# A third level of Strassen for one of the seven small products of a half product, in groups 1 to 3

## The chip, the cores and the metric

The kernel runs on one core of one Trainium2 chip. The metric is the device time of one execution in microseconds. The kernel before was timed three times on the chip: 819.81, 819.81 and 819.62 us, median 819.81 us. A profile of one further execution gives the start and length of every instruction.

## The reference

The input `x` has 4 x 1024 rows of 1024 floats. The rows are normalised, and two things are made of them: a gated recurrence along the rows of a sequence (its gate is `sigmoid(xn @ gate_w.T + gate_b)`), and a network whose outputs are added, by their top-2 expert numbers 0 to 7, into eight rows only. As `silu(0)` is 0, all other rows of the result are `x`, and the recurrence is needed for the first sequence alone.

```python
xn = _layernorm(x, axis=-1)
# attention-like part
g   = sigmoid(einsum('btd,ed->bte', u, gate_w) + gate_b);  u_g = u * g
y   = c * s + d_eff * u_g                    # s: cumulative sum along the sequence; d_eff: needs the mean of u_g
# network part, on all 4096 rows of xn
gates = top-2 of softmax(xr @ wr.T), renormalised
h = silu(xr @ w1.T);  h = silu(h @ w3.T);  h = h @ w2.T
out = out.at[indices_k[:, k]].add(gates[:, k:k+1] * h)
# result
return x + y * silu(out)
```

Nearly all the arithmetic lies in three products with a 1024 x 1024 matrix: `w1` and `w3` for all 4096 rows, `gate_w` for the first 1024 rows. All of it is in float32.

## The kernel before

**Groups and half products.** The 4096 rows ("tokens") are worked in four groups of 1024, numbered `sb` = 0 to 3. Each group has a product with `w1` (kind `u`), then a product with `w3` (kind `m`); group 0 also has the one with `gate_w` (kind `g`). A 1024 x 1024 x 1024 product is made by one level of Strassen (the Winograd form) as seven products of 512 x 512 x 512; the source calls each a `Half` and names it by its number `i`. `u` takes them in the order 1, 2, 5, 6, 7, 4, 3 and `m` in the order 1, 5, 6, 2, 7, 4, 3.

**Seven steps of a half.** Each half is made by a second level of Strassen, so by seven products of 256 x 256 x 256. One such product is one step on TensorE: four matmuls with 128 x 128 weights and 256 moving columns (function `small`, line 869). In float32 the profile records each matmul as two weight loads and two matmul records, so a step is eight records. `Half.step(n)` (line 919) runs step n. Steps 0, 2, 4 and 6 add into one PSUM bank, X; steps 1 and 5 into another, Z; step 3 makes its product alone in the bank Y. X and Z have two buffers each, Y has one (lines 104 to 106), and with the others all eight PSUM banks are in use.

**Reading the banks out.** After most steps VectorE adds the bank, as far as it has been summed, to a 128 x 512 quarter of the output block in SBUF: `first` (line 904) for quarters 0, 3, 1 and 2 after steps 0, 1, 2 and 6, and `more` (line 913) for quarters 0, 3 and 1 after steps 3, 4 and 5. In halves 1 and 5 the reads of `first` are copies on ScalarE. Step 3 is `go(Y, A[:, 1], t[:, 2], True, True)` and then `self.more(0, Y)`. In halves 6 and 7 every finished quarter is followed by one more VectorE addition between output blocks (`whole`, line 1005), and a finished quarter of a final block goes through SiLU on ScalarE (`done`).

**Operands.** The sums that the second level needs are made by GpSimd on the token side (`left_sums`, 128 x 512 subtractions and additions); the weight sums were made in group 0, stored to DRAM, and are loaded again for groups 1 to 3 (`load_kept` 1 MB, `load_kept_sum` 256 KB each). The token sums of the first level (`s1` to `s4`) run on GpSimd for `u` in groups 1 to 3 and on VectorE for `m`. While the `m` product of group 1 or 2 runs, VectorE also normalises the tokens of the next group, in 16 operations of 128 x 1024 (`norm`, line 407). All 128 x 512 operands live in a ring of `NQ` = 18 tiles ("quarters"), taken from the front and given back at the end; 1 MB blocks live in a ring of 20.

**Order.** The order of work on every engine is written out by the program. Each half has a starting place S, seven places after the half before it; its step n runs at place S + 2n. So steps 4, 5 and 6 of the half before fall at S + 1, S + 3 and S + 5, between the steps 0 to 3 of this one, and each place holds one step. Other work is put on a list with `at(place, function)`; whatever is due at a place is issued before the step of that place (`run_todo`, lines 186 to 201, and the loop at line 1421). Each engine then keeps exactly that order, and waits when an operand or a buffer is not ready. The route of the next group's tokens (`route`, line 439: two transposes, VectorE maxima, a sigmoid on ScalarE, VectorE comparisons) is spread over such places during the first halves of `u`.

Of the kernel before, what the change touches and what calls it, by code (L numbers as in the profile page):

```python
# [10 lines left out]
F32 = mybir.dt.float32  # L11
# [3 lines left out]
ALU = mybir.AluOpType  # L15
AX = mybir.AxisListType
P = 128
Q = 256
# [4 lines left out]
def kernel(  # L23
# [55 lines left out]
    class Pinned:  # L79
# [15 lines left out]
    nc = tc.nc  # L95
    pe, dve, act, pool, sync = (
        Pinned(e) for e in (nc.tensor, nc.vector, nc.scalar, nc.gpsimd, nc.sync)
    )
# [7 lines left out]
    ps_y = ctx.enter_context(tc.tile_pool(name="ps_y", bufs=1, space=bass.MemoryType.PSUM))  # L106
# [15 lines left out]
            if self.uses == 0:  # L122
                self.home.append(self.tile)

    NB, NQ = 20, 18
    IDLE = 13
    blocks = deque(
        const.tile([P, 4, 2 * Q], F32, tag=f"b{i}", name=f"b{i}") for i in range(NB)
# [8 lines left out]
    def quarter(uses=1):  # L137
        return Held(quarters, uses)
# [47 lines left out]
    def at(place, f, *args):  # L186

        seq[0] += 1
        heapq.heappush(todo, (place, seq[0], f, args))
# [8 lines left out]
    def resume(p, g):  # L198
        step = next(g, None)
        if step is not None:  # L200
            at(p + step, resume, p + step, g)
# [14 lines left out]
    start = {}  # L216
# [301 lines left out]
    kept = {}  # L518
    op_t = {}
# [14 lines left out]
    def keep_quarter(name, i, j, o):  # L534
        d = dramp.tile([P, 2 * Q], F32, tag=f"{name}_{i}_{j}", name=f"{name}_{i}_{j}")
        sync.dma_start(d, o.tile)
        kept[name, i, j] = d
        o.drop()
# [177 lines left out]
    def first_w3():  # L716
# [48 lines left out]
    S_OF = {  # L765
        1: (0, 0),
        2: (0, 1),
        4: (1, 1),
        5: "s1",
        6: "s2",  # L770
        3: "s4",
        7: "s3",
    }
    left = {}
# [91 lines left out]
                yield 2 * (A_AT[j + 1] - A_AT[j])  # L866


    def small(ps, A, B, start, stop, rows_first):

        for mt in range(2):
            for kt in range(2):
                w, m = (A, B) if rows_first else (B, A)
                pe.matmul(
                    ps[:, mt * Q : (mt + 1) * Q],
                    w[:, kt * Q + mt * P : kt * Q + (mt + 1) * P],
                    m[:, kt * Q : (kt + 1) * Q],
                    start=(start and mt == 0 and kt == 0),
                    stop=(stop and mt == 1 and kt == 1),
                    skip_group_check=True,  # L880
                )
# [3 lines left out]
    class Half:  # L885
# [30 lines left out]
        def whole(self, q):  # L916
            whole(self.kind, self.sb, self.i, q)

        def step(self, n):
            if n == 0:  # L920
                self.begin()
            A, t = self.A, self.t
            ts = [op_ts.get((self.kind, self.sb, self.i, j)) for j in range(4)]
            s = [left_q.get((self.src, self.sb, self.i, j)) for j in range(4)]

            def go(ps, a, b, start, stop):
                small(ps, a, b, start, stop, self.rows_first)

            if self.plain:

                q = ((0, 1, 2, 3) if self.i == 1 else (0, 3, 1, 2))[n // 2]
                ps = self.X if n // 2 % 2 == 0 else self.Z
                go(ps, A[:, q // 2 * 2 + n % 2], t[:, n % 2 * 2 + q % 2], n % 2 == 0, n % 2 == 1)
                if n % 2:
                    self.first(q, ps)
            elif n == 0:
                go(self.X, A[:, 0], t[:, 0], True, False)
                self.first(0, self.X)
            elif n == 1:
                go(self.Z, s[0].tile, ts[0].tile, True, False)  # L940
                self.first(3, self.Z)
                s[0].drop()
                ts[0].drop()
            elif n == 2:
                go(self.X, s[1].tile, ts[1].tile, False, False)
                self.first(1, self.X)
                s[1].drop()
                ts[1].drop()
            elif n == 3:
                Y = ps_y.tile([P, 2 * Q], F32, tag="Y", name=f"Y_{self.tag}")  # L950
                go(Y, A[:, 1], t[:, 2], True, True)
                if (self.kind, self.i) == ("g", 1):
                    at(Y_AT, self.more, 0, Y)
                else:
                    self.more(0, Y)
            elif n == 4:
                go(self.X, s[2].tile, ts[2].tile, False, False)
                self.more(3, self.X)
                s[2].drop()
                ts[2].drop()  # L960
            elif n == 5:
                go(self.Z, s[3].tile, t[:, 3], False, True)
                self.more(1, self.Z)
                s[3].drop()
            elif n == 6:
                go(self.X, A[:, 3], ts[3].tile, False, True)
                self.first(2, self.X)
                self.whole(2)
                ts[3].drop()
            if n == (7 if self.plain else 6):  # L970
                self.A.drop()
                t.drop()
# [265 lines left out]
    for kind, sb, i, plain in line:  # L1238
        h = Half(kind, sb, i, plain)
        halves.append(h)  # L1240
        S = start[kind, sb, i]
        n = 2 if sb == 0 and kind == "u" and i not in PLAIN_G else 1
        if kind != "g" and not plain:
            at(S + 2 - 8, left_sums, kind, sb, i, n)
        if kind != "g" and sb > 0:
            at(S - 10, load_kept, kind, sb, i)
            for j in range(4):
                at(S + 2 * T_AT[j] - 9, load_kept_sum, kind, sb, i, j)

    for sb in range(NS):  # L1250
        n = 2 if sb == 0 else 1
# [252 lines left out]
```

## Time and profile before

| what | us |
|---|---|
| median of 3 runs (lowest, highest) | 819.81 (819.62, 819.81) |
| span of the profiled execution | 817.9 |
| what lies around the span, against the median | 1.9 |
| one step on TensorE, 8 records, distance to the next step | 1.73 |
| VectorE, PSUM bank Y + SBUF, 128 x 512, mean of one | 0.69 |
| VectorE, `whole` and first-level sums, 128 x 512, mean of one | 0.93 |
| VectorE, normalising, 128 x 1024, mean of one | 1.21 |
| GpSimd, 128 x 512 sum, mean of one | 1.31 to 1.36 |
| load of a 256 KB weight sum, issue to landing, median | 4.5 |

The profiled execution's own time is known by its span; the three timed runs lie 1.7 to 1.9 us above that. A page of the profile gives the busy time of each engine, the chain of work that ended last, and the costliest groups of instructions; the timeline lists instructions of one engine in order of time, as "start, length, engine, line, operation, output<-inputs, shape, how many in a row". Nearly all instructions are recorded by one helper (line 89), so they are told apart by their tiles: `b` is a 1 MB block, `q` a quarter, `X_u`, `Z_m`, `Y_m` and so on the PSUM banks of the halves, `bc` the normalisation's factors.

### The profile page before, as it was taken

Reading aid. Unit: us, or ns where it says so; the run is one execution under the profiler, and the core shown is the slowest. Engines: PE = TensorE matmul, PEld = TensorE weight load, DVE = VectorE, ACT = ScalarE, POOL = GpSimd, SP = SyncE. Lnnn points to the kernel's source line nnn. Section 1 sums busy time; section 2 is a strip of 40 time slices with the busy share of each in tenths; the row PEclk is TensorE's granted clock in tenths of the full one; section 3 lists DMA queues with packets and bytes.
Section 4 is the critical chain, followed back from the end, with each engine's and each line's share of the span. In section 5 each row is a group of like instructions: output and inputs, shape, how many; then the busy total and the mean of one; then the engine's idle time right before and its main releaser. Section 6 shows DMA issues by size and latency. Waiting matters only on the chain.

```text
span 817.9 us, 11299 instructions
## 1 busy us (share of the span) xinstructions
PE 810.6 (99%) x4085; PEld 696.5 (85%) x4085; DVE 509.7 (62%) x868; ACT 263.8 (32%) x458; POOL 496.1 (61%) x398
## 2 busy tenths in 40 slices
PE   8999999999999999999999999999999999999997
PEld 7888888888888878888888788888888788888885
DVE  6886598765588524764985235666983246667643
ACT  1245126877232237341022065421122021220111
POOL 2799896967999394744547453755448454465300
PEclk9999999999999999999999999999999999999999
DMA  9946619465978947629955875559666365555700
GB/s 338 421 175 232 230 47 357 171 246 160 411 267 309 345 174 293 241 103 385 376 179 210 332 279 190 187 206 426 242 244 257 104 219 203 196 180 195 283 14 2
DMA packets 55927, 192.88 MB, mean 236 GB/s; under 512 B 6480, under 2 KB 9792, under 8 KB 44224
## 3 DMA queue, kind: packets, MB, share of 16 engines
q1 hardware_dynamic: 55552, 191.61, 63.5%
q8 instruction: 33, 0.54, 0.3%
q10 hardware_dynamic: 320, 0.54, 0.2%
q14 instruction: 22, 0.18, 0.1%
HBM read 169.01 MB, written 39.87 MB: 255 GB/s over the span
## 4 chain that ended last, share of the span: by engine, by line
PE 98%; DMA 1%; DVE 0%; ACT 0%; issue 0%; SPq 0%
PE X_u L89 24%; PE X_m L89 24%; PE Z_u L89 12%; PE Z_m L89 12%; PE X_g L89 6%; PE Y_m L89 6%; PE Y_u L89 6%; PE Z_g L89 3%; PE acc L89 2%; PE plT L89 2%; PE Y_g L89 1%; DMA b<-in_x 1%; PE pp L89 0%; DVE bn L89 0%; PE accB L89 0%; PE ta L89 0%
## 5 line engine op out<-in xcount | busy, mean ns | idle before, releaser
L89 POOL TENSOR_TENSOR q<-b 128x512 f32<-128x512 f32 x154 | 203.0, 1331 | 193.7 <-PE X_m L89 48.0
L89 ACT ACTIVATE b<-b 128x512 f32<-128x512 f32 (+1 forms) x152 | 105.3, 696 | 298.1 <-DVE b L89 291.6
L89 POOL TENSOR_TENSOR q<-b,q 128x512 f32<-128x512 f32 x98 | 133.1, 1361 | 7.2 <-issue 4.0
L89 POOL TENSOR_TENSOR b<-b,b 128x512 f32<-128x512 f32 x72 | 92.9, 1310 | 48.5 <-PE X_u L89 33.7
L89 DVE TENSOR_TENSOR b<-b,b 128x512 f32<-128x512 f32 x120 | 109.2, 925 | 2.7
L89 PE MATMUL X_m<-q,q 128*128 128x256 f32 x448 | 105.9, 379 | 0.0
L89 PE MATMUL X_u<-q,q 128*128 128x256 f32 x432 | 102.4, 380 | 0.0
L89 DVE TENSOR_TENSOR b<-X_u,b 128x512 f32<-128x512 f32 x87 | 60.0, 690 | 57.8 <-PE X_u L89 57.1
L89 DVE TENSOR_TENSOR b<-X_m,b 128x512 f32<-128x512 f32 x88 | 60.4, 688 | 56.9 <-PE X_m L89 56.7
L89 PEld LDWEIGHTS X_m<-q,q 128*128 128x128 f32 x448 | 85.0, 190 | 12.4 <-issue 0.8
L89 POOL TENSOR_TENSOR q<-q,b 128x512 f32<-128x512 f32 x56 | 73.6, 1314 | 32.4 <-PE X_u L89 25.1
L89 PEld LDWEIGHTS X_u<-q,q 128*128 128x128 f32 x432 | 81.8, 190 | 12.2 <-issue 1.2
L89 DVE TENSOR_TENSOR b<-b,bc 128x1024 f32<-128x1024 f32 x56 | 67.8, 1211 | 0.1
L89 PE MATMUL X_u<-b,b 128*128 128x256 f32 x248 | 58.4, 380 | 0.0
L89 PE MATMUL Y_m<-b,b 128*128 128x256 f32 x224 | 53.1, 380 | 0.0
L89 PE MATMUL Z_m<-b,q 128*128 128x256 f32 x224 | 53.0, 380 | 0.0
L89 PE MATMUL X_m<-b,b 128*128 128x256 f32 x224 | 53.0, 379 | 0.0
L89 PE MATMUL Z_m<-q,q 128*128 128x256 f32 x224 | 52.9, 379 | 0.0
L89 PE MATMUL X_m<-q,b 128*128 128x256 f32 x224 | 52.9, 379 | 0.0
L89 PEld LDWEIGHTS X_u<-b,b 128*128 128x128 f32 x248 | 47.0, 190 | 6.7 <-DVE b L89 0.4
L89 DVE TENSOR_TENSOR b<-Z_u,b 128x512 f32<-128x512 f32 x47 | 32.4, 690 | 31.6 <-PE Z_u L89 30.7
L89 PE MATMUL Z_u<-q,q 128*128 128x256 f32 x216 | 51.1, 380 | 0.0
(182 smaller groups left out, 1171.6 us busy)
## 6 DMA issues: line engine op xcount, KB each, us to landing
q<-w SPq DMA_DIRECT2D x168, 256.0 KB, 4.5
b<-in_w SPq DMA_DIRECT2D x36, 1024.0 KB, 9.0
b<-w_T SPq DMA_DIRECT2D x24, 1024.0 KB, 6.3
b<-in_xT SPq DMA_DIRECT2D x15, 1024.0 KB, 12.9
w<-q SPq DMA_DIRECT2D x56, 256.0 KB, 7.4
b<-in_x SPq DMA_DIRECT2D x12, 1024.0 KB, 11.0
w_T<-b SPq DMA_DIRECT2D x8, 1024.0 KB, 4.4
b<-in_gw SPq DMA_DIRECT2D x6, 1024.0 KB, 14.0
```

The source lines that it names most:

```text
L89: r = f(*args, **kwargs)
```

## The change

Step 3 of every half of kinds `u` and `m` in groups 1 to 3 (42 halves) is no longer four matmuls of 256 columns. Its 256 x 256 x 256 product is made by seven products of 128 x 128 x 128, each a matmul of 128 columns, in the same bank Y. They are spread over four points, called `eighth(0)` to `eighth(3)`: one matmul at S + 1, two at S + 3, one at S + 5, and three at S + 6, where step 3 was. VectorE reads the bank after each: 128, 256 and 128 columns, and at the end twice 256; these five additions take the place of the one of 512 columns. GpSimd makes four 128-column sums of the tokens per half (`token_thirds`, three instructions), and in group 1 four of the weights (`weight_thirds`), which are stored (256 KB a half) and loaded again in groups 2 and 3 (`load_thirds`). The ring of quarters grows from 18 to 24 tiles, for which the memory kept for GpSimd's descriptors is cut to 1024.

```diff
-    NB, NQ = 20, 18
+    NB, NQ = 20, 24
...
+    def is_third(kind, sb, i):
+        return sb > 0 and kind != "g"
+
+    def cut(t):
+        return t.rearrange("p (k n) -> p k n", n=P)
+
+    def token_thirds(kind, sb, i):
+        a = cut(left[kind, sb, S_OF[i]][:, 1])
+        t = quarter()
+        o = cut(t.tile)
+        third_s[kind, sb, i] = t
+        pool.tensor_tensor(
+            o[:, 0:2], a[:, 1:2].to_broadcast([P, 2, P]), a[:, 0::3], ALU.subtract
+        )
+        yield 1
+        pool.tensor_tensor(o[:, 2], a[:, 0], o[:, 1], ALU.subtract)
+        pool.tensor_tensor(o[:, 3], a[:, 2], o[:, 2], ALU.subtract)
+
+    def weight_thirds(kind, sb, i):
+        name = {"u": "w1", "m": "w3"}[kind]
+        b = cut(op_t[kind, sb, i][:, 2])
+        t = quarter(2)
+        o = cut(t.tile)
+        third_t[kind, sb, i] = t
+        pool.tensor_tensor(o[:, 1], b[:, 1], b[:, 0], ALU.subtract)
+        yield 1
+        pool.tensor_tensor(o[:, 2], b[:, 3], o[:, 1], ALU.add)
+        pool.tensor_tensor(o[:, 3], b[:, 2], o[:, 2], ALU.subtract)
+        yield 1
+        pool.tensor_tensor(o[:, 0], b[:, 1], b[:, 3], ALU.add)
+        yield 1
+        keep_quarter(name, i, "t", t)
+
+    def load_thirds(kind, sb, i):
+        o = quarter()
+        sync.dma_start(o.tile, kept[{"u": "w1", "m": "w3"}[kind], i, "t"])
+        third_t[kind, sb, i] = o
...
+        def eighth(self, n):
+            key = self.kind, self.sb, self.i
+            a, b = cut(self.A[:, 1]), cut(self.t[:, 2])
+            S, T = cut(third_s[key].tile), cut(third_t[key].tile)
+            d = cut(self.dst[:, 0])
+            z, w = (1, 2) if self.rows_first else (2, 1)
+            if n == 0:
+                self.Y = ps_y.tile([P, 2 * Q], F32, tag="Y", name=f"Y_{self.tag}")
+            ps = cut(self.Y)
+            def go(o, p, q, start, stop):
+                left_side, right_side = (p, q) if self.rows_first else (q, p)
+                pe.matmul(
+                    ps[:, o], left_side, right_side, start=start, stop=stop, skip_group_check=True
+                )
+            def add(o, p):
+                dve.tensor_add(o, p, o)
+            if n == 0:
+                go(3, a[:, 0], b[:, 0], True, False)
+                add(d[:, 0], ps[:, 3])
+            elif n == 1:
+                go(z, S[:, 1], T[:, 1], False, False)
+                go(0, a[:, 2], b[:, 2], False, False)
+                add(d[:, 0::3], ps[:, 0 : z + 1 : z])
+            elif n == 2:
+                go(3, S[:, 2], T[:, 2], False, False)
+                add(d[:, z], ps[:, 3])
+                self.z = z
+            else:
+                go(3, S[:, 0], T[:, 0], False, True)
+                go(z, S[:, 3], b[:, 3], False, True)
+                go(w, a[:, 3], T[:, 3], False, True)
+                add(d[:, w::3-w], ps[:, 3:4].to_broadcast([P, 2, P]))
+                add(d[:, 1:3], ps[:, 1:3])
+                third_s[key].drop()
+                third_t[key].drop()
+                self.whole(0)
...
+            elif n == 3 and is_third(self.kind, self.sb, self.i):
+                self.eighth(3)
             elif n == 3:
...
+        if is_third(kind, sb, i):
+            for n, step in enumerate((1, 3, 5)):
+                at(S + step, h.eighth, n)
+            at(S - 1, token_thirds, kind, sb, i)
+            at(S - 3, *((weight_thirds if sb == 1 else load_thirds), kind, sb, i))
...
-    nc = bacc.Bacc("TRN2", target_bir_lowering=False, num_devices=1)
+    nc = bacc.Bacc("TRN2", target_bir_lowering=False, num_devices=1, dynamic_dma_scratch_size=1024)
```

More of the change, by code (lines that the diff above doesn't have):

```diff
@@ L866, in left_sums @@
                 yield 2 * (A_AT[j + 1] - A_AT[j])
+    third_s = {}
+    third_t = {}
+    def is_third(kind, sb, i):
[31 more added lines that the diff above has]
+        third_t[kind, sb, i] = o
     def small(ps, A, B, start, stop, rows_first):
```

## The prediction

> **What bounds the kernel now.** I read the page first.
>
> ```profile
> span 817.9 us, 11299 instructions
> ...
> PE 810.6 (99%) x4085; PEld 696.5 (85%) x4085; DVE 509.7 (62%) x868; ACT 263.8 (32%) x458; POOL 496.1 (61%) x398
> ...
> PEclk9999999999999999999999999999999999999999
> ...
> PE 98%; DMA 1%; DVE 0%; ACT 0%; issue 0%; SPq 0%
> ```
>
> TensorE is busy for 99% of the span at the full clock, and the chain that ended last is TensorE for 98%. Then its waits, in all:
>
> ```profile
> PE idle L89 <- POOL eps L89: 1.6, 1, 1.6
> PE mean L89 <- DVE mv L89: 0.7, 1, 0.7
> PE scale L89 <- DVE rs L89: 0.3, 1, 0.3
> PE pp L89 <- DVE accT L89: 0.3, 1, 0.3
> ```
>
> Three are at the start, one at the very end: between the first half product and the last TensorE never waits. Whatever shortens its stream shortens the kernel, and any wait put into it costs in full. So I price first the stream, then each new wait.
>
> **The stream.** A step of eight records of 256 columns takes 1.73 us from start to start (403.46, 405.18, 406.91 below), 216 ns a record. For 128 columns in float32 the nearest row is the warm-up product at the full clock:
>
> ```profile
> 8.64 0.75 PEld L89 LDWEIGHTS idle<-ident,ones 128*128 128x128 f32 x6
> ...
> 8.75 0.83 PE L89 MATMUL idle<-ident,ones 128*128 128x128 f32 x6
> ```
>
> The last of the six takes 0.275 us, so the other five lie (0.83 - 0.275)/5 = 111 ns apart, each with its weight load. Seven products are 14 records: 14 x 0.112 = 1.57 us for 1.73, 0.16 us a half, 6.7 us for 42 halves. Returning from 128 columns to 256 cost 4 ns after the transposes near 805.6 us; four returns a half make 0.7 us. Gain: 6.0 us. Bounds for a record are 109 ns (the four transposes there, 0.60 us) and 118 ns (the four `ta` matmuls, different weights each, 0.61 us with 0.256 for the last): a gain of 7.3 to 2.5 us.
>
> The Trainium skill speaks against this step: TensorE: Matmul & The Clock Gate, section "Back-to-back issue gap", says that in a stream of load and matmul pairs a 128-column matmul costs about 81 ns where it alone would take 56. By that ratio a record would be 162 ns, a half 0.54 us longer, and the stream 23 us longer instead of 6 shorter. The row above has loads between all its matmuls and shows 111 ns, so I go by the row.
>
> **The new waits.** Y has one buffer. Before, it was written at S + 6 and next at S + 13. Now it is in use from S + 1 to S + 6 and the next half's `eighth(0)` wants it at S + 8, one step after `eighth(3)`. VectorE must by then have finished the two closing additions, and it works strictly in order: behind the previous half's step 6 read, its `whole`, and whatever first-level sums or normalising stand there. Everything behind `eighth(0)` on TensorE waits too.
>
> Clearance: let E be the end of the matmuls of the previous half's step 6. Its last record starts 0.38 before E; then come 0.216, `eighth(3)` 6 x 0.112 = 0.67, and the next half's step 0, 1.73. `eighth(0)` is due 2.24 us after E. The additions take 0.84: a 128x256 VectorE operation with a PSUM operand is 0.42 (`b<-b,scale`), and these two depend on each other. From VectorE's end to a restarted matmul I take 0.165 (the first X_u: VectorE ends at 9.56, the record starts at 9.62 and is 0.10 longer than its 0.38; bounds 0.06 by the start alone, 0.18 by the first `pp` after `accT`, 810.57 to 810.75). If VectorE is free D after E, TensorE waits D + 0.84 + 0.165 - 2.24 = D - 1.23 us. In 18 of the 42 places D is the read alone, 0.73, or less, and nothing waits; in 21 the queue is longer, and three (m 6) come with the second clearance below. The worst, half m 2 of group 1:
>
> ```profile
> 403.46 1.89 PE L89 MATMUL X_m<-q,b 128*128 128x256 f32 x8
> 405.18 1.89 PE L89 MATMUL Y_m<-b,b 128*128 128x256 f32 x8
> 406.91 1.89 PE L89 MATMUL X_m<-b,b 128*128 128x256 f32 x8
> ...
> 405.60 0.68 DVE L89 TENSOR_TENSOR b<-X_m,b 128x512 f32<-128x512 f32 x1
> 406.38 0.97 DVE L89 TENSOR_TENSOR b<-b,b 128x512 f32<-128x512 f32 x1
> 407.28 1.21 DVE L89 TENSOR_TENSOR b<-b,bc 128x1024 f32<-128x1024 f32 x1
> 408.41 1.28 DVE L89 TENSOR_TENSOR b<-b,b 128x512 f32<-128x512 f32 x2
> 409.62 0.68 DVE L89 TENSOR_TENSOR b<-Y_m,b 128x512 f32<-128x512 f32 x1
> ```
>
> E = 405.35. Read, `whole`, normalising and two first-level sums end at 409.69, D = 4.34: 3.1 us of wait. Today Y is read 2.5 us late here and nobody needs the bank. Half u 5 is another kind, VectorE held by ScalarE:
>
> ```profile
> 306.63 1.89 PE L89 MATMUL X_u<-b,q 128*128 128x256 f32 x8
> ...
> 308.63 0.69 DVE L89 TENSOR_TENSOR b<-X_u,b 128x512 f32<-128x512 f32 x1 [0.58 <-PE X_u L89]
> 311.72 0.23 DVE L89 TENSOR_TENSOR oh<-pl,ix 128x64 f32<-128x64 f32 x1 [2.40 <-ACT pl L89]
> ...
> 310.00 1.28 ACT L89 ACT_TABLE_LOAD   x1
> ```
>
> The route's comparison, just ahead of the additions, waits for a SiLU, a table load and a sigmoid: E = 308.52, D = 3.43, wait 2.2. The same reading of all 42 places gives:
> - u 5, three groups, D 3.35 to 3.43: 6.4 us.
> - m 2: D 4.34 in groups 1 and 2, 2.84 in group 3 (no normalising): 6.2 + 1.6.
> - m 4: D 2.59 (read, `whole`, normalising), twice, and 1.45: 2.7 + 0.2.
> - m 7 of groups 1 and 2 and u 1 of group 1: D 1.86 (read, normalising): 1.9.
> - u 7, D 1.90 (a `whole` of 1.06 beside GpSimd); u 3, D 1.93 (two first-level sums); u 4, D 1.47; three groups each: 2.0 + 2.1 + 0.7.
>
> Sum 23.8 us in 21 places. A second clearance: `eighth(3)` needs the bank that VectorE reads after `eighth(2)`, one step earlier. It is due 1.79 after the end of step 2's matmuls (0.216 + 0.224 + 1.73 - 0.38); the read costs 0.25 to 0.29 behind the read of X. In half m 6 of groups 1 and 2 that read ends 3.76 after its matmuls (normalising and sums before it; 395.27 against 391.51), in group 3 2.31: 2.4 + 2.4 + 0.95, and 0.4 over m 2 and m 4: 6.1 us. Waits in all: 30 us. The closing additions may take 0.76 to 0.96, the restart as bounded above, over 21 places: 26 to 33.
>
> **What I cost at nothing.** *VectorE's own load*: five additions for one, 0.29 + 0.42 + 0.29 + 0.42 + 0.42 - 0.69 = 1.15 us a half (0.29 lies between 128x64, 0.21, and 128x256, 0.42), 48 us on an engine with 308 idle; counted only by the queues above, though it can lengthen them where VectorE is nearly full (half m 6, about 0.4 twice). *GpSimd*: 512 columns of sums a half, as much again in group 1, by the 1.31 us of a 128x512 sum 56 x 1.3 = 74 us in 322 idle; by the 128x128 memset row, 0.20, they could be near 45. Its sums lie ahead of their use: in half u 4 of group 1, tightest, GpSimd is held by a first-level sum until 334.0, the first token sum ends near 334.7, and `eighth(1)` wants it near 339.4; 4.7 us are left. If that cover goes, TensorE waits for the difference. *DMA*: 42 x 256 KB, 11 MB on 193. A load at S - 3 is used at S + 3, six steps or 10.4 us later, against 4.5 us to land; on SP's queue it stands among the other quarter loads, and six more tiles let that queue run further ahead than the two tiles per half take away.
>
> **Sum.** 817.9 - 6.0 + 30 = 841.9 us of span, and with the 1.9 us between span and median 843.8. By bounds: stream -7.3 to -2.5, waits 26 to 33, so 838 to 850.
>
> **Rivals.**
> - *The cover holds* (faster). If the bank is handed on before VectorE's last read, or VectorE is ahead at these places, only the stream counts: 813.8 us. For it: not one TensorE wait today. Against: one Y buffer, and D is read from rows. It decides once the waits sum to less than 6 us, under 0.3 us in each of 21 places. 6%.
> - *Half the waits.* One wait gives VectorE time, so the queue behind it is shorter: 15 us of waits, 829 us. For it: m 2 follows m 6, and both waits have one backlog. Against: sums and normalising stand in program order behind the reads and move with them. 10%.
> - *GpSimd joins.* From 333 to 351 us it is busy 16.6 of 18 us; the added sums of one and a half halves (3.9 us in group 1) overfill the window, and its slower neighbours lengthen VectorE's `whole` (0.69 alone, up to 1.80 beside it). 3 us a group, 9 in all: 853 us. 12%.
> - *Weight loads not covered.* If a record costs the 190 ns its load is recorded with, the stream grows by 14 x 0.19 - 1.73 = 0.93 us a half, 39 us; `eighth(3)` then takes 0.47 longer and eases 21 waits by 10: 879 us. Against: the row of six above. 3%.
>
> **How the numbers follow.** The forecast, 838 to 850, has 69%; it is the likeliest, 843.8. To leave out no more than two in ten, the range goes down to the half-wait case and up past GpSimd's: 828 to 855. A difference under 0.2%, 1.6 us, cannot be told from none here. Slower 0.92 (forecast, half, GpSimd and loads, less a little of the half case), same 0.02, faster 0.06.
>
> **What would show it.** TensorE's waits list VectorE for Y_u and Y_m, some 25 times, about 30 us, longest near 3 us, at m 2, m 6 and u 5 above all; TensorE's busy time falls to about 804; 128-column records 112 ns apart; no waits for q tiles of GpSimd or DMA. I am wrong if Y's first matmul follows step 0 without a gap in half m 2, or if the records lie 160 ns apart.

## The result and the profile after

The changed kernel takes 853.66 us (median of 4 runs, 851.39 to 854.69) where the kernel before takes 819.71 us in runs beside it: 1.0405 times as long, 95% interval 1.0388 to 1.0422. It is slower by 34 us. The profiled execution spans 851.6 us, 33.7 more than before.

The page of the changed kernel: span, busy time of each engine with its share and number of instructions, the granted clock of TensorE in 40 slices, and the shares of the chain that ended last.

```profile
span 851.6 us, 12354 instructions
...
PE 820.0 (96%) x4337; PEld 700.4 (82%) x4337; DVE 553.6 (65%) x1036; ACT 263.5 (31%) x458; POOL 591.9 (70%) x580
...
PEclk9999999999999999999999999999999999999999
...
PE 85%; DVE 12%; issue 1%; ACT 1%; DMA 1%; SPq 0%; DVEq 0%
```

VectorE, 0% of the chain before, now has 12% of it, though it is busy for only 65% of the span. So TensorE waits for VectorE at places, not because VectorE is full on the average. The waits of TensorE, as "bank <- who is waited for: us in total, times, longest":

```profile
PE Y_m L89 <- DVE b L89: 14.6, 13, 2.2
PE Y_u L89 <- DVE oh L89: 4.5, 3, 1.5
...
PE X_m L89 <- DVE b L89: 0.8, 2, 0.5
...
PE Y_u L89 <- DVE b L89: 0.3, 2, 0.2
```

Bank Y leads, as foreseen: `oh` is the route's comparison, three times, which the prediction has as u 5 (it names a wait by the half whose closing additions come late; the waiting `eighth(0)` is that of the next half). But this list adds up to some 20 us, and 33.7 + 6 us have to be found. A wait shows there only where TensorE is idle. A matmul record of 256 columns is 0.38 us long and the next one starts 0.216 after it, so the last 0.16 us of a stretch hides as much of a wait, and the first record after a wait is recorded 0.08 to 0.10 longer. I therefore counted each wait as the distance between two records beyond its usual value (0.216 us after 256 columns, 0.112 after 128), where that is over 0.03 us. Before, this sum is 1.4 us; in the changed kernel it is 41.7. So 40.3 us were lost, and the stream itself gained 40.3 - 33.7 = 6.6. All sums of waits below are counted in this way.

| where TensorE loses time | us | places |
|---|---|---|
| bank Y at `eighth(0)` | 17.5 | 19 |
| bank X at step 0 of the next half | 12.0 | 35 |
| bank Y at `eighth(3)` | 9.0 | 10 |
| records at a lower clock | 1.7 | 1 |
| all else, with the 1.4 of before | 1.5 | |

The second line is in no term of the prediction. The start of half u 4 of group 1 (the prediction's u 7) shows it together with the first. TensorE's timeline of the changed kernel, as "start, length, engine" and so on:

```profile
333.86 1.89 PE L89 MATMUL X_u<-b,q 128*128 128x256 f32 x8
335.59 0.39 PE L89 MATMUL Y_u<-q,q 128*128 128x128 f32 x2
335.81 0.39 PE L89 MATMUL Y_u<-q,b 128*128 128x128 f32 x2
336.03 0.39 PE L89 MATMUL Y_u<-b,q 128*128 128x128 f32 x2
336.54 1.99 PE L89 MATMUL X_u<-b,b 128*128 128x256 f32 x8
338.59 0.46 PE L89 MATMUL Y_u<-b,b 128*128 128x128 f32 x2
```

and VectorE's in the same stretch:

```profile
335.79 0.69 DVE L89 TENSOR_TENSOR b<-X_u,b 128x512 f32<-128x512 f32 x1 [1.06 <-PE X_u L89]
336.58 1.06 DVE L89 TENSOR_TENSOR b<-b,b 128x512 f32<-128x512 f32 x1
337.57 0.87 DVE L89 TENSOR_TENSOR b<-Y_u,b 128x256 f32<-128x256 f32 x2
```

The first TensorE row is step 6 of the half before last, into bank X; then come the three matmuls of `eighth(3)`, 0.67 us; and step 0 of the next half wants the same bank, since X has two buffers and the other one is in use. It is due at 336.25, but VectorE reads that bank from 335.79 to 336.48, and step 0 starts at 336.54. When step 3 was 1.73 us long, the read ended well ahead of it. Most of the 35 places lose 0.38 us in this way (counting the slower start of the next record, 0.10), and 0.27 where ScalarE does the reading. Below it stands the wait that was forecast: the `whole` of 1.06 holds up the two closing additions, which end at 338.44, and `eighth(0)`, due at 338.37 behind the late step 0, starts at 338.59.

### The profile page after: what moved, and what is told of

Read it like the earlier page. It is cut to its first block, busy times and chain, and to the rows that moved or that the text cites. A ratio compares the mean times of both kernels' runs of the same rounds, so it can differ in the third digit from the quotient of the medians.

```text
span 851.6 us, 12354 instructions
## 1 busy us (share of the span) xinstructions
PE 820.0 (96%) x4337; PEld 700.4 (82%) x4337; DVE 553.6 (65%) x1036; ACT 263.5 (31%) x458; POOL 591.9 (70%) x580
## 4 chain that ended last, share of the span: by engine, by line
PE 85%; DVE 12%; issue 1%; ACT 1%; DMA 1%; SPq 0%; DVEq 0%
PE X_u L89 22%; PE X_m L89 18%; PE Z_u L89 12%; DVE b L89 12%; PE Z_m L89 10%; PE X_g L89 6%; PE Y_u L89 4%; PE Y_m L89 4%; PE Z_g L89 3%; PE acc L89 2%; PE plT L89 2%; PE Y_g L89 1%; DMA b<-in_x 1%; ACT L89 0%; PE pp L89 0%
## 5 line engine op out<-in xcount | busy, mean ns | idle before, releaser
L89 POOL TENSOR_TENSOR q<-b 128x512 f32<-128x512 f32 (+2 forms) x224 | 250.4, 1129 | 135.3 <-PE Y_m L89 30.6
L89 POOL TENSOR_TENSOR q<-b,q 128x128 f32<-128x128 f32 (+1 forms) x210 | 189.5, 905 | 18.1 <-PE X_u L89 6.3
L89 DVE TENSOR_TENSOR b<-b,b 128x512 f32<-128x512 f32 x120 | 111.8, 945 | 2.7
L89 DVE TENSOR_TENSOR b<-Y_m,b 128x256 f32<-128x256 f32 (+2 forms) x112 | 43.3, 387 | 32.3 <-PE Y_m L89 24.9
L89 DVE TENSOR_TENSOR b<-Y_u,b 128x256 f32<-128x256 f32 (+2 forms) x111 | 42.7, 384 | 32.6 <-PE Y_u L89 22.9
L89 PE MATMUL X_u<-b,b 128*128 128x256 f32 x248 | 60.3, 387 | 1.6 <-DVE b L89 0.2
## 6 DMA issues: line engine op xcount, KB each, us to landing
b<-in_w SPq DMA_DIRECT2D x36, 1024.0 KB, 13.5
```

Source lines behind the costliest of these rows:

```text
L89: r = f(*args, **kwargs)
```

## The experiments

Each edit is made in the changed kernel. The sum of waits is beside each time.

**The work beside TensorE alone.** All that runs on GpSimd and the queues stays, with the larger ring; step 3 is again four matmuls and one read, so the added sums are made and not used.

```diff
-            elif n == 3 and is_third(self.kind, self.sb, self.i):
-                self.eighth(3)
             elif n == 3:
+                if is_third(self.kind, self.sb, self.i):
+                    third_s[self.kind, self.sb, self.i].drop()
+                    third_t[self.kind, self.sb, self.i].drop()
...
-            for n, step in enumerate((1, 3, 5)):
-                at(S + step, h.eighth, n)
```

> Side work alone: GpSimd's sums of the third level, their stores and loads and the ring of 24 tiles as in the changed kernel, but step 3 is again four matmuls of 256 columns and one VectorE read, so the sums are made and not used. If the loss comes from banks that VectorE hands over late, none of it is left: 819 to 821 us, and TensorE's waits list nothing between the first half and the last. If GpSimd's 96 us of added work, the 11 MB of added transfers or the sharing between GpSimd and VectorE cost something of their own, it shows here: 823 us or more, with waits for q tiles or slower VectorE additions.

821.34 us against 819.69, ratio 1.0021 (1.0012 to 1.0031); waits 2.7 us, the new ones at step 0 of m 7. The sums, stores, loads and tiles cost 1.6 us of the 34. All else comes with `eighth` itself.

**Step 6 one place earlier.** Step 6 of the half before is put ahead of step 2, so that VectorE has a whole step more to read bank X; `eighth(2)` moves with it, to stay apart from `eighth(3)`.

```diff
-            for n, step in enumerate((1, 3, 5)):
+            for n, step in enumerate((1, 3, 3.2)):
...
-        (at_first[kind, sb, i][n] if (kind, sb, i) in at_first else start[kind, sb, i] + 2 * n, k, n)
+        (at_first[kind, sb, i][n] if (kind, sb, i) in at_first else start[kind, sb, i] + 2 * n - (1.5 if n == 6 and sb > 0 else 0), k, n)
```

> The changed kernel with step 6 of each half in groups 1 to 3 run one and a half places earlier (before step 2 of the next half instead of after it), and eighth(2) at S + 3.2. Step 6's read of bank X then has a whole step and eighth(3) before step 0 of the half after next wants that bank. If step 0's wait of 0.38 us in nearly every half is for that read, its 12 us go, and as the queue behind step 6 now has 1.73 us more before the closing additions, most of the waits on Y go too: 816 to 821 us. If step 0 waits for an operand (its waits list loads as well), its 12 us stay: 826 us or more.

844.65 us, waits 29.5 in the profiled execution, which took 841.76. The wait for bank X at step 0 fell from 12.0 to 0.4 us: its cause is shown. The 9.0 us at `eighth(3)` fell to 0.3 as well. But the time was expected near 818, and that was wrong: `eighth(0)` now waits 22.4 us in place of 17.5. What step 0 and `eighth(3)` had waited ahead of it was in part the same lateness of VectorE, paid earlier. At half m 4 of group 1, for example, `eighth(3)` and the `eighth(0)` of the next half had waited 0.9 us each; now that `eighth(0)` alone waits 1.8. `eighth(1)` and `eighth(2)` wait 3.4.

**`eighth(0)` one step later.** The alternative cure: bank Y is wanted one step later, step 6 stays. `eighth(2)` is moved as in the run before.

```diff
-            for n, step in enumerate((1, 3, 5)):
+            for n, step in enumerate((2, 3, 3.2)):
```

> The changed kernel with eighth(0) one place later (S + 2) and eighth(2) earlier (S + 3.2), step 6 left where it was. Bank Y then has one more step between the closing additions and its next use, and two between eighth(2) and eighth(3). If the waits on Y are VectorE handing over the bank, the 26 us fall to 2 to 4 (only half m 2, whose queue is 4.3 us long, is still late), the clock does not drop, and the 12 us of step 0 stay: 825 to 830 us. If the stream of 128-column matmuls is itself slower, little changes: above 840 us.

843.88 us, waits 32.0. `eighth(0)` waits only 2.0 us in place of 17.5, so its wait was the short distance, as forecast, and `eighth(3)` only 0.3; bank X at step 0 keeps 13.5 us. Slower than expected, for a new reason: `eighth(1)` and `eighth(2)` now wait 15.1 us, and `eighth(1)` each time until 0.10 to 0.15 us after VectorE's read of the result of `eighth(0)`.

**Both moves.** Step 6 as in the one, the three points as in the other run.

> Both moves: step 6 one and a half places earlier, eighth(0) at S + 2, eighth(2) at S + 3.2. If the loss is the waits on Y and X and nothing else, only the shorter stream is left, about 6.6 us: 812 to 816 us, faster than the kernel before. If the stream gains nothing or side work costs, 818 us or more.

832.77 us, ratio 1.0158 (1.0141 to 1.0175), waits 20.5: X 0.9, `eighth(0)` 4.2, `eighth(1)` and `eighth(2)` 12.9. The two moves roughly add up (844 and 845 alone, 833 together), but the sum misses the expected 812 to 816 by the new wait.

**Who makes `eighth(1)` wait.** This is made on top of both moves. The trace named GpSimd's tiles for some of these waits. If the token sums were late, making them two places earlier would help; if VectorE's read of the result of `eighth(0)` was what is waited for, it would not.

```diff
-        yield 1
+        yield 0
...
-            at(S - 1, token_thirds, kind, sb, i)
-            at(S - 3, *((weight_thirds if sb == 1 else load_thirds), kind, sb, i))
+            at(S - 3, token_thirds, kind, sb, i)
+            at(S - 5, *((weight_thirds if sb == 1 else load_thirds), kind, sb, i))
```

> Both moves of the run before (832.8 us), and GpSimd's sums earlier: all four token sums of a half issued together at S - 3, the weight sums and their loads at S - 5. In that run TensorE still waited 12.9 us at eighth(1) and eighth(2), 4.2 us at eighth(0). If those 12.9 us are GpSimd's second and third token sums, which stood behind sums of the second level that wait for buffers, they go: 819 to 822 us. If they are VectorE's reads of bank Y in the halves where VectorE is full (m 6, 2, 7, 4), at most half goes: 826 us or more.

838.95 us, and `eighth(1)` and `eighth(2)` wait 14.1 us in place of 12.9. Late sums are not the cause. The trace of both moves says the same: 25 of its waits at `eighth(1)` and `eighth(2)` end 0.10 to 0.15 us after VectorE's read of the piece before, also where the list names GpSimd; only two of 0.2 us have no such read near them. Of the 6 us by which the time rose, 5.6 are found in TensorE's records (1.5 us more of waits at `eighth(0)`, 1.6 at bank X, 1.2 at `eighth(1)` and `eighth(2)`, and 1.3 at a lower clock); why they came was not followed up.

**Without the halves where VectorE is fullest**, m 6, 2, 7 and 4, on top of the last edit (30 halves are left).

```diff
-        return sb > 0 and kind != "g"
+        return sb > 0 and kind != "g" and not (kind == "m" and i in (6, 2, 7, 4))
```

> The same, but halves m 6, 2, 7 and 4 keep the step 3 of the kernel before; in groups 1 and 2 VectorE is busy there for 10.5 to 11.5 of 12.1 us. The third level is left in 30 halves. If what is left of the loss is VectorE having no room there, only the shorter stream of the 30 halves and under 2 us of waits remain: 815 to 818 us, faster than the kernel before. If the loss were spread over all halves, it would be 12/42 smaller than in the run before and the time still above 819.

823.51 us, waits 9.6, of them 4.4 at `eighth(1)` and `eighth(2)`. Most of the waits belonged to the twelve halves left out, but the time is above the expected 815 to 818.

**The first two points in one.** The matmul of `eighth(0)` is issued together with the two of `eighth(1)`, and VectorE reads after all three, so no matmul stands behind a read of a part of its own bank. It is made on top of both moves, in all 42 halves.

```diff
-            if n == 0:
+            if n == 1:
                 go(3, a[:, 0], b[:, 0], True, False)
-                add(d[:, 0], ps[:, 3])
-            elif n == 1:
                 go(z, S[:, 1], T[:, 1], False, False)
                 go(0, a[:, 2], b[:, 2], False, False)
+                add(d[:, 0], ps[:, 3])
                 add(d[:, 0::3], ps[:, 0 : z + 1 : z])
...
-            for n, step in enumerate((2, 3, 3.2)):
+            for n, step in ((1, 2), (2, 3.2)):
```

> The run with both moves (832.8 us) showed TensorE at eighth(1) waiting until VectorE had read what eighth(0) wrote, although they use different columns of Y. Here the matmuls of eighth(0) and eighth(1) are issued together at S + 2 and read after them; eighth(2) stays at S + 3.2 and eighth(3) at S + 6, so that each of the three uses of the bank has two steps before the next. If the 12.9 us at eighth(1) and eighth(2) are that hand-over, most go: 819 to 823 us, the rest in halves m 6, 2, 7, 4 where VectorE is full. If they are GpSimd's sums being late, the time stays at 831 us or rises, because the sums are now needed one place earlier.

823.78 us against the 832.77 of both moves, waits 11.4 against 20.5. The same half u 4 shows why. TensorE's timeline with both moves:

```profile
338.38 0.38 PE L89 MATMUL Y_u<-b,b 128*128 128x128 f32 x2
338.60 1.89 PE L89 MATMUL Z_u<-q,q 128*128 128x256 f32 x8
340.62 0.46 PE L89 MATMUL Y_u<-q,q 128*128 128x128 f32 x2
```

VectorE's in the same run:

```profile
339.31 0.97 DVE L89 TENSOR_TENSOR b<-b,b 128x512 f32<-128x512 f32 x1
340.20 0.28 DVE L89 TENSOR_TENSOR b<-Y_u,b 128x128 f32<-128x128 f32 x1
```

`eighth(0)` is long done, VectorE comes to its result after a `whole`, at 340.20, and `eighth(1)`, due at 340.33, starts 0.14 us after that read has ended, though it writes other columns of the bank. (A token sum of GpSimd ends at 340.59 there. It is not what is waited for: the same matmul starts at 338.70 in the next rows, before that sum is even begun.) TensorE's with the points in one:

```profile
338.48 0.38 PE L89 MATMUL Y_u<-b,b 128*128 128x128 f32 x2
338.70 0.39 PE L89 MATMUL Y_u<-q,q 128*128 128x128 f32 x2
338.93 0.39 PE L89 MATMUL Y_u<-b,b 128*128 128x128 f32 x2
339.15 1.89 PE L89 MATMUL Z_u<-q,q 128*128 128x256 f32 x8
```

and VectorE's:

```profile
340.32 0.73 DVE L89 TENSOR_TENSOR b<-Y_u,b 128x128 f32<-128x128 f32 x2
```

VectorE is as late as before and nobody waits. That a read of one part keeps a matmul out of another part is what the Trainium skill would lead one to: PSUM — Partial Sum Buffer, section "PSUM bank collisions raise a hardware error", says that TensorE and VectorE must not access one bank on the same partitions at once, disjoint columns included. The rows above agree, 0.14 us from the read's end to the matmul. By the same section the hardware does not make an engine wait in such a case, so the waiting is done by the program's semaphores; no run here shows what would happen without them.

**The same without the full halves**: m 6, 2, 7 and 4 keep the four matmuls (30 halves).

> The same in 30 halves, with step 3 as before in m 6, 2, 7 and 4. If only bank hand-overs stood against the shorter stream, 30 x 0.157 = 4.7 us less than the kernel before and 1 to 2 us of waits more: 815 to 818 us, faster than the kernel before. If side work costs what its own run showed (1.6 us) on top, 817 to 819 us.

818.15 us (11 runs) against 819.71 (16 runs), ratio 0.9981 (0.9972 to 0.9990), waits 4.0. This is faster than the kernel before, by 1.6 us or 0.2%. Its page:

```profile
span 816.6 us, 11999 instructions
...
PE 807.9 (99%) x4265; PEld 698.7 (86%) x4265; DVE 539.6 (66%) x988; ACT 263.0 (32%) x458; POOL 563.3 (69%) x528
```

TensorE is at 99% again. The span is 1.3 below that of before with 2.6 us more of waits, so 30 halves save 3.9 us, 0.13 each.

**In group 3 all halves again** (34 halves). While `m` of group 3 runs, VectorE has no next group to normalise. The weight sums of the four halves are made in group 3 itself.

```diff
-        return sb > 0 and kind != "g" and not (kind == "m" and i in (6, 2, 7, 4))
+        return sb > 0 and kind != "g" and not (kind == "m" and sb < 3 and i in (6, 2, 7, 4))
```

> As the run with the merged first points and 30 halves, but the halves m 6, 2, 7 and 4 of group 3 have the third level again (34 halves; their weight sums are made in group 3). In the merged run with 42 halves the TensorE waits in group 3 were under 0.4 us each, since no normalising for a next group stands on VectorE there. Theory (VectorE's normalising is what makes these halves wait): no new waits, four halves save 0.13 us each, so 817.6 us, 0.5 below the 818.15 of the run with 30 halves. Rival (these halves wait for VectorE's first-level sums alone, wherever they are): 819 us or more, with waits at Y_m in group 3.

818.17 us, ratio 0.9979 (0.9970 to 0.9989), waits 4.1: no new wait over 0.1 us in group 3, as the theory has it. The expected gain of 0.5 us is not seen in the times; the span is 0.3 shorter.

**In groups 1 and 2 only m 2 and m 7 left out** (38 halves).

```diff
-        return sb > 0 and kind != "g" and not (kind == "m" and sb < 3 and i in (6, 2, 7, 4))
+        return sb > 0 and kind != "g" and not (kind == "m" and sb < 3 and i in (2, 7))
```

> As the run before, but in groups 1 and 2 only m 2 and m 7 stay without the third level (38 halves). In the merged run with 42 halves the waits in m 7 were 2.6 and 1.5 us and those in m 6 and m 2 0.2 to 0.6. Theory (each wait belongs to the half that shows it): about 0.2 us of waits for m 6 and some 0.5 us less of stream, so 817 to 818 us. Rival (VectorE is full there, and its five additions in m 6 and m 4 push the backlog into whatever comes next): the waits move to X, Z or to m 4 and the time is 819 us or more.

819.85 us, ratio 1.0001 (0.9992 to 1.0010), waits 6.7: here the rival was right. The third level in m 6 makes a wait of 1.6 us in the half after it, m 2, which has no third level; with m 6 left out too, in the two runs before, there was none. Another 0.7 us, at m 6 of group 2, the list of waits puts down to a late load of the weight sums. TensorE's timeline at m 2 of group 1:

```profile
412.16 1.89 PE L89 MATMUL Z_m<-b,q 128*128 128x256 f32 x8
415.43 1.99 PE L89 MATMUL X_m<-q,b 128*128 128x256 f32 x8 [1.38 <-DVE b L89]
```

and VectorE's:

```profile
409.49 2.58 DVE L89 TENSOR_TENSOR b<-b,b 128x512 f32<-128x512 f32 x2
412.00 0.68 DVE L89 TENSOR_TENSOR b<-Y_m,b 128x512 f32<-128x512 f32 x1
412.60 1.57 DVE L89 TENSOR_TENSOR b<-b,b 128x512 f32<-128x512 f32 x1
414.10 1.28 DVE L89 TENSOR_TENSOR b<-X_m,b 128x512 f32<-128x512 f32 x2
```

VectorE runs without a gap here, and TensorE goes on 0.05 us after the second read of X has ended at 415.38. A wait in one half can be owed to work put into the half before.

## Why the prediction was right, and where it was short

The direction and the mechanism were right: one Y buffer, wanted too soon after VectorE's closing additions, in a kernel whose TensorE had no slack. The rival that the cover holds was rightly put low. The size was too small: the time, 853.66, lies above the forecast proper, 838 to 850, and inside the range of 828 to 855 only because that had been stretched for a rival with another cause (GpSimd). That part is luck. Against the predicted span of 841.9 the measured one is 9.7 longer, and step by step:

- *The stream*: -6.0 predicted, -6.6 found, as what is left when the waits are taken off the span. Records of 128 columns lie 0.11 us apart (335.59, 335.81 and 336.03 above, for two records each), and 42 x (1.73 - 14 x 0.112) is 6.8. By the section of the Trainium skill weighed there (TensorE: Matmul & The Clock Gate, "Back-to-back issue gap") the stream would have grown by an estimated 23 us; the measurement decides against it.
- *`eighth(0)`*: 23.8 us predicted in 21 places. In the 19 places found, TensorE waits 17.5 us at `eighth(0)` and 6.8 at the step 0 just ahead of it, 24.3 in all. What VectorE's lateness costs was read rightly from the trace of before: the two parts together are 0.67 us each at u 7 (predicted 2.0 for three), 2.1 to 2.2 each at u 5 (predicted 6.4 for three), and 3.0, 3.0 and 2.1 at m 2 (predicted 3.1, 3.1 and 1.6). Smaller places agree less well: m 4 gave 1.8 for 2.9, u 4 1.6 for 0.7. It is only paid in two parts, the first at bank X.
- *`eighth(3)`*: 6.1 predicted, 9.0 found. This term was too small: the waits at m 6 in groups 1 to 3 were 0.6, 2.1 and 1.9 (predicted 2.4, 2.4 and 0.95), and m 2 and m 4 gave 4.2 in place of 0.4. VectorE, held by its own added pieces and by neighbours on GpSimd, was later there than the rows of before said; which of the two was not separated.
- *Bank X, the term that is missing*: the prediction worked out when bank Y comes free and took it for the only bank that the change touches. But making step 3 shorter by 1.06 us also brings the next step 0 that much closer to step 6, whose bank it reuses. Cost: 5.2 us in the places where `eighth(0)` would not have waited anyway (12.0 less 6.8). The run with step 6 moved shows the cause.
- *The clock*: 1.7 us, not foreseen, told below.
- *The sum*: 0.5 + 2.9 + 5.2 + 1.7 - 0.6 = 9.7 us. It closes because the stream is the remainder.
- *What was costed at nothing*: GpSimd's added work was sized 74 us and is 96 (591.9 less 496.1). It was nevertheless hidden, as said; with the DMAs and the ring it costs 1.6 us. VectorE's pieces have the predicted durations, 0.42 and 0.29, but their place matters more: the run with the points in one shows 9 us for it.
- *TensorE's busy time* was to fall to 804 and rose to 820.0. Each of the 64 breaks adds up to 0.26 us to it (0.16 of a record that no successor overlaps, 0.10 by which the first record after it is longer), at most 17 us, and the lower clock 1.7. It was a bad sign to choose.

The rival with GpSimd, 853 us, has the measured time but not the cause: the run with the side work alone shows 1.6 us and the run with earlier sums no gain.

## What to carry to other kernels

When a step on a full engine is made shorter, work out the release of every buffer whose next use comes closer by it, not only of the buffer that the edit names. Where a bank was written in pieces and read in pieces, each matmul waited for the read before it, so group the writes ahead of the reads. A change that wins 0.13 us a half where VectorE has time pays only there: leave it out where VectorE runs without a gap, and out of the half ahead of such a place too.

## What the runs showed of the hardware

**The clock can fall after short waits.** Busy time of the changed kernel by stretches (us and number of instructions for PE, PEld, DVE, ACT and POOL; then the granted clock, the DMA share and GB/s):

```profile
410.00:414.00 4.00, 2.20 (x13) 1.53 (x12) 3.90 (x7) 0.00 (x0) 3.84 (x6) 1.00 0.89 364
414.00:418.00 4.00, 1.83 (x10) 1.33 (x9) 3.96 (x7) 0.33 (x1) 0.82 (x1) 1.00 0.61 205
418.00:420.00 2.00, 2.00 (x8) 1.68 (x8) 1.13 (x3) 0.79 (x2) 1.14 (x1) 0.63 0.04 8
420.00:422.00 2.00, 2.00 (x6) 1.56 (x6) 0.71 (x2) 0.00 (x0) 1.66 (x4) 0.51 0.00 0
422.00:424.00 2.00, 2.00 (x13) 1.82 (x12) 1.69 (x2) 0.63 (x1) 1.14 (x2) 1.00 0.39 131
```

and the rows behind it:

```profile
412.33 0.49 PE L89 MATMUL Y_m<-q,q 128*128 128x128 f32 x2 [1.45 <-DVE b L89]
...
413.62 1.99 PE L89 MATMUL X_m<-b,b 128*128 128x256 f32 x8 [0.36 <-DVE b L89]
417.78 0.46 PE L89 MATMUL Y_m<-b,b 128*128 128x128 f32 x2 [2.17 <-DVE b L89]
418.08 3.17 PE L89 MATMUL X_m<-q,q 128*128 128x256 f32 x8
```

After waits of 1.45, 0.36 and 2.17 us the clock is granted at half for some 3.4 us, and a step takes 3.0 us in place of 1.73; that adds 1.7 us to the waits. In the run with the points in one, a single wait of 2.36 us (first row below) did the same. Other waits did not: those of 1.82 us before 590.31 and 2.02 before 608.10 left the clock of the changed kernel at 1.00, and so did one of 3.00 in the run with step 6 earlier (second row):

```profile
413.27 0.46 PE L89 MATMUL Y_m<-b,b 128*128 128x128 f32 x2 [2.36 <-DVE b L89]
...
602.54 0.46 PE L89 MATMUL Y_m<-b,b 128*128 128x128 f32 x2 [3.00 <-DVE b L89]
```

It also differs between executions of one kernel: the four with step 6 earlier took 841.8 to 845.2 us, at mean granted clocks of 0.998 to 0.992. The Trainium skill, TensorE: Matmul & The Clock Gate, section "Part 1: The HAM clock gate", lets the clock fall to half after an idle window of about 3.4 us; no gap of the changed kernel or of the run with the points in one was that long, so the measurement adds that shorter waits can be enough. The length of one wait alone does not decide it (2.36 us were enough once, 3.00 were not); what does was not tried.

**GpSimd's small sums are dear.** Groups of the changed kernel by shape (count, busy us, mean ns, idle before):

```profile
L89 POOL TENSOR_TENSOR q<-b 128x512 f32<-128x512 f32 x154 | 201.5, 1316 | 117.5 <-PE Y_m L89 30.6 <-DVE b L89 24.0 <-PE X_m L89 15.9
...
L89 POOL TENSOR_TENSOR q<-b,q 128x128 f32<-128x128 f32 x112 | 59.8, 534 | 5.4
L89 POOL TENSOR_TENSOR q<-b 128x256 f32<-128x256 f32 x42 | 34.6, 825 | 14.0 <-PE X_u L89 7.1 <-PE X_m L89 5.6 <-issue 0.7
```

A quarter of the columns takes 534 ns of 1316, or 41%. By an estimate from these two rows about 0.27 us of each is there whatever the size (534 less a third of the 782 ns by which four times the columns take longer); the row of 256 columns, 825 ns, fits it to 0.03 us.
